# Two pauses in the scatters of rows 16 to 31 of an attention and expert kernel

## The chip, the cores and the metric

The kernel runs on one core of one Trainium2 chip. The metric is the device time of one execution in microseconds (us); where several executions are compared, the median is taken. A core has a matrix engine (PE, with its weight loads shown apart as PEld), three engines for element-wise work (DVE, ACT, POOL), and a queue engine for transfers (SP). ACT and POOL issue transfers too. All transfers run on the same 16 DMA engines of the core.

## The reference

The input holds 4 images of 32 channels, 128 x 128. Each is folded into a matrix of 128 channels by 4096 positions, or 4096 tokens of 128 values as the second layer sees it. Cut to what matters:

```python
# layer 0: attention between channels
q = xs.reshape(B, 128, 4096)
energy = jnp.einsum('bci,bcj->bij', q, q)        # 4096 x 4096 per image
d = jnp.sqrt(jnp.diagonal(energy, axis1=1, axis2=2))
attn = jax.nn.softmax(energy / (d[:, :, None] * d[:, None, :]), axis=-1)
x = gamma * jnp.einsum('bcj,bij->bci', q, attn) + xs
# layer 1: linear attention, then 2 of 8 experts for each token
t = tokens(x)
t = t + linear_attention(layernorm(t), Wk, Wq, Wv)
n = layernorm(t)
top_p, top_i = top_k(softmax(n @ router_w + router_b), 2)
top_p = top_p / sum(top_p)
t = t + sum over the two of  top_p * (n @ expert_w[top_i] + expert_b[top_i])
```

## The kernel before

**Attending.** `attend(b)` walks over the 4096 x 4096 energies of image b in tiles of 128 x 512, row block after row block (0 to 7). One step makes the energies of a tile on PE (`pe`, L556), their exponentials on ACT (`pr`, L559), and two steps later their product with the values (`po`, L440). The energies are symmetric, so only the tiles up to the diagonal are made. The transposed part of a tile goes another way: DVE transposes `pr` in blocks into `F` (L369), SP stores F to DRAM as `blocks` (L483), SP loads it back in another order as `G`, in four quarters (L491), and PE multiplies it (`pg`, L375) while ACT sums its rows (`junk`, L380). The products with G stand LAG = 57 units of the kernel's own clock behind the load. In the last row block of the last image F goes to G directly, in 16 transfers (L476).

**Closing.** When 84% of an image is attended, `layer1(b)` starts as a second stream. Every PACE = 10 units of the clock it makes one step, a "turn" in what follows, while the same image and then the next one are attended. It divides and adds (`close_rows`, L700 to L744), forms the linear attention, and then runs four threads, `attention_rows(u)` for 8 rows of 128 tokens each, started one after another. Threads 1 and 3 end in `sorted_experts(0)` for rows 0 to 15 and `sorted_experts(1)` for rows 16 to 31, for images 0 to 2. Image 3, the last, has no next image to hide behind and multiplies all tokens with all experts instead (`last_parts`).

**Sorting.** `sorted_experts(h)` handles 16 rows with two choices each, 32 pieces. It computes the place of each token in a list ordered by expert, and scatters the 32 pieces to DRAM with indexed transfers from POOL (L995, `xs`), two for every two turns. Each scatter waits for the exponentials of its step. When the thread has issued all, it notes "moved". Then 20 pairs of tiles are loaded by SP (L1019), transposed (L1062) and multiplied by the expert's weights (L1055) on PE, copied by ACT and DVE (L1029, L1038) and stored by SP (`ys`, L1041). At last POOL gathers 32 pieces back (L1120, `yb`), DVE adds them in with their weights (L1089, "combine"), for groups of four rows whose sum starts with a fetch on ACT's queue (`acc`, L1096) and ends with four stores on SP (L1102). Rows 16 to 31 do not start their scatters before rows 0 to 15 have "moved" and do not gather before those have "gathered"; rows 0 to 15 do not gather before rows 16 to 31 have "moved".

**Order.** The orders of PE, DVE, ACT and SP are those in which the program issues its instructions (`manual_schedule`); on POOL the gathers, scatters and small chains are kept in order too (`pinned`). All streams are interleaved by the clock, which counts matmul work, and not by measured time. A pause moves what follows in its thread against all other work, and with it the place in each engine's list. The threads of `stagger` each make a step per turn.

The transfers of SP and ACT draw their completion semaphores from a ring of eight, in the program's order, so a transfer waits until the one eight places ahead of it has landed. The groups of four rows take turns in three `acc` tiles, so a fetch waits for the stores of the group three before. The POOL scatters and gathers have a ring of eight of their own.

Of the kernel before, what the change touches and what calls it, by code (L numbers as in the profile page):

```python
# [22 lines left out]
def kernel(  # L23
# [105 lines left out]
    def wait_for(inst, others, why):  # L129
        for other in others:  # L130
            tc.add_manual_dep(
                inst, other.name, mybir.DependencyInfo(mybir.DependencyClass.Sync, mybir.DependencyReason.DATA),
                reason=why,
            )
# [24 lines left out]
    def pinned(inst):  # L159
        tc.keep_in_program_order(inst)  # L160
        return inst
# [16 lines left out]
    def idle(n):  # L178
        for _ in range(2 * n):
            yield  # L180
# [421 lines left out]
    def layer1(b, st):  # L602
# [276 lines left out]
        def attention_rows(u):  # L879
# [32 lines left out]
            if u % 2:  # L912
                for _ in route(u // 2):
                    yield
                    yield
                yield
                yield
                yield from sorted_experts(u // 2)

        def sorted_experts(h):  # L920
# [66 lines left out]
            def offset(ap):  # L987
                return bass.IndirectOffsetOnAxis(ap=ap, axis=0)
# [4 lines left out]
            for n in range(2 * HR):  # L993
                k, i = r0 + n // 2, n % 2
                inst = nc.gpsimd.indirect_dma_start(xs[h], offset(place[:, i, k : k + 1]), xn[:, k, :], None)  # L995
                if not scatters:
                    pinned(inst)
                else:
                    tc.declare_no_dep(inst.ins, group=f"scatter_{b}_{h}", reason="no two tokens have the same place")
                tc.add_to_no_dep_group(f"scatter_{b}_{h}", inst.ins)  # L1000
                wait_for(inst.ins, xs_made[h] + xs_read[h], "what is replaced was made and read before")
                wait_for(inst.ins, exps, "not more of these at a time than steps have")
                scatters.append(inst.ins)
                if n % 2:
                    yield
                    yield
            turns[h].append("moved")
            xs_made[h][:], xs_read[h][:] = scatters, []
            yield from idle(3)
# [402 lines left out]
```

## Time and profile before

| what | value |
|---|---|
| five runs | 1725.01, 1728.0, 1727.58, 1729.35, 1726.7 us, median 1727.58 |
| the profiled execution | 1721.76 us, span 1720.0 us, granted clock 0.99 |
| busy, share of the span | PE 96%, DVE 54%, ACT 54%, POOL 30% |
| scatters L995 | 192, 968 ns each on POOL |
| gathers L1120 | 192, 962 ns each on POOL |
| transfers | 355.25 MB, 207 GB/s over the span |

A busy time is how long an engine's instructions ran. A row of 40 digits cuts the span into 40 equal parts, each with its busy share in tenths. A wait is named by the engine and line that waited and by what it waited for. "SPq" and "ACTq" are the queues from which SP and ACT issue transfers. Issuing and moving are two things: the time shown beside an issue is that of the engine's queue. Times such as 708.64 us count from the start of the span. In image 0 the scatters of rows 16 to 31 lie at 552 to 604 us, the gathers of rows 0 to 15 at 655 to 707 us and those of rows 16 to 31 from 709 us on; images 1 and 2 repeat this some 412 and 820 to 825 us later.

### The profile page before, as it was taken

Reading aid. Unit: us, or ns where it says so; the run is one execution under the profiler, and the core shown is the slowest. Engines: PE = TensorE matmul, PEld = TensorE weight load, DVE = VectorE, ACT = ScalarE, POOL = GpSimd, SP = SyncE. Lnnn points to the kernel's source line nnn. Section 1 sums busy time; section 2 is a strip of 40 time slices with the busy share of each in tenths; the row PEclk is TensorE's granted clock in tenths of the full one; section 3 lists DMA queues with packets and bytes.
Section 4 is the critical chain, followed back from the end, with each engine's and each line's share of the span. In section 5 each row is a group of like instructions: output and inputs, shape, how many; then the busy total and the mean of one; then the engine's idle time right before and its main releaser. Section 6 shows DMA issues by size and latency. Waiting matters only on the chain. (4 is left out here: it accounts for less than half of the span.)

```text
span 1720.0 us, 21208 instructions
## 1 busy us (share of the span) xinstructions
PE 1656.7 (96%) x5458; PEld 877.8 (51%) x5458; DVE 934.4 (54%) x2443; ACT 925.8 (54%) x2893; POOL 510.4 (30%) x553
## 2 busy tenths in 40 slices
PE   8999999999999999999999999999999999999897
PEld 4444444455654455445554455544555445544643
DVE  4433334467585235577478334557748633455686
ACT  3545445466565455446565545545657545544476
POOL 1000000011026505540015631653102661354156
PEclk9999999999999999999999999999999999999999
DMA  4675777866569899995569879998557979996001
GB/s 134 197 208 171 205 221 236 260 207 184 176 194 269 248 257 263 260 259 164 160 195 243 266 221 258 282 254 232 173 157 193 277 237 259 268 262 161 1 10 41
DMA packets 240681, 355.25 MB, mean 207 GB/s; under 512 B 27312, under 2 KB 155312, under 8 KB 226480
## 3 DMA queue, kind: packets, MB, share of 16 engines
q1 hardware_dynamic: 220048, 314.91, 64.2%
q0 software_dynamic: 12288, 25.19, 5.0%
q10 hardware_dynamic: 8224, 13.77, 2.7%
q8 instruction: 46, 0.75, 0.2%
q14 instruction: 75, 0.61, 0.1%
HBM read 183.64 MB, written 173.15 MB: 207 GB/s over the span
## 5 line engine op out<-in xcount | busy, mean ns | idle before, releaser
L559 ACT ACTIVATE pr<-pe 128x512 f32<-128x512 f32 (+1 forms) x576 | 322.4, 560 | 566.8 <-PE pe L556 433.8
L440 PE MATMUL po<-pr,qT 128*128 128x512 f32 (+3 forms) x1152 | 554.3, 563 | 3.9 <-ACT o L445 3.4
L556 PE MATMUL pe<-qn,qn 128*128 128x512 f32 x896 | 461.9, 597 | 4.2 <-ACT pr L559 3.9
L375 PE MATMUL pg<-G,qT 128*128 128x512 f32 x880 | 452.3, 596 | 9.4 <-DMA G<-blocks 9.4
L369 DVE STREAM_TRANSPOSE F<-pr 128x512 f32<-128x512 f32 x440 | 306.0, 702 | 154.6 <-ACT pr L559 130.8
L440 PEld LDWEIGHTS po<-pr,qT 128*128 128x128 f32 x1152 | 216.7, 192 | 251.2 <-issue 225.2
L380 ACT ACTIVATE junk<-G 128x512 bf16<-128x512 f32 x440 | 272.9, 620 | 2.9 <-DMA G<-blocks 2.6
L375 PEld LDWEIGHTS pg<-G,qT 128*128 128x128 f32 x880 | 167.7, 192 | 208.8 <-issue 192.5
L1120 POOL DMA_INDIRECT yb<-ys,place x192 | 184.8, 962 | 261.4 <-DMA ys<-result 97.2
L995 POOL DMA_INDIRECT xs<-xn,place x192 | 185.8, 968 | 133.0 <-ACT pr L559 55.7
L556 PEld LDWEIGHTS pe<-qn,qn 128*128 128x128 f32 x896 | 154.6, 191 | 116.1 <-issue 102.9
L385 DVE TENSOR_TENSOR o<-o,pg 128x512 f32<-128x512 f32 x110 | 75.4, 685 | 208.8 <-PE pg L375 162.7
L164 POOL TENSOR_TENSOR rn<-ss,neg_half 128x8 f32<-128x8 f32 (+1 forms) x17 | 26.9, 1585 | 333.4 <-DVE ss L325 333.3
L559 ACT ACTIVATION_READ_ACCUMULATOR pr<-pe 128x1 f32 x576 | 112.1, 195 | 0.0
L1029 ACT ACTIVATE xn<-pys 128x256 f32<-128x256 f32 (+1 forms) x120 | 45.0, 378 | 111.9 <-PE pys L1062 63.5
L1055 PEld LDWEIGHTS pys<-ew_sb,xn 128*128 128x128 f32 x468 | 68.9, 193 | 54.8 <-issue 39.6
L164 POOL TENSOR_TENSOR rsf<-dm_f,neg_half 128x8 f32<-128x8 f32 (+1 forms) x15 | 26.2, 1747 | 235.2 <-DVE sv_f L636 235.2
L556 PE MATMUL pe<-qn 128*128 128x512 f32 (+3 forms) x256 | 90.9, 438 | 0.7 <-ACT qn L344 0.7
L164 POOL TENSOR_TENSOR rsa<-dm_a,neg_half 128x8 f32<-128x8 f32 x16 | 26.4, 1649 | 218.0 <-DVE sv_a L636 217.7
L380 ACT ACTIVATION_READ_ACCUMULATOR junk<-G 128x1 f32 x440 | 84.3, 192 | 0.0
L1055 PE MATMUL pys<-ew_sb,xn 128*128 x468 | 71.9, 277 | 10.0 <-ACT xn L1029 9.6
L1038 DVE COPY result<-pys 128x256 f32<-128x256 f32 (+1 forms) x60 | 24.6, 410 | 97.3 <-ACT xn L1029 41.8
(212 smaller groups left out, 1606.9 us busy)
## 6 DMA issues: line engine op xcount, KB each, us to landing
blocks<-F SPq DMA_DIRECT2D x108, 1024.0 KB
G<-blocks SPq DMA_DIRECT2D x432, 256.0 KB
xn<-xs SPq DMA_DIRECT2D x114, 128.0 KB
below<-F SPq DMA_DIRECT2D x31, 384.0 KB
G<-below SPq DMA_DIRECT2D x124, 96.0 KB
out_dram<-acc SPq DMA_DIRECT2D x128, 64.0 KB
xx<-in_x_dram SPq DMA_DIRECT2D x62, 128.0 KB
ys<-xn SPq DMA_DIRECT2D x60, 128.0 KB
```

The source lines that it names most:

```text
L164: pinned(nc.gpsimd.tensor_tensor(dst, src, neg_half.to_broadcast(list(src.shape)), ALU.pow))
L369: f()
L375: nc.tensor.matmul(pg.rearrange("p (a f) -> p a f", a=4), st["qT"][i][:, ib, :], G[:, :, ib], start=(ib == 0), stop=(ib == NJ - 1),)
L380: nc.scalar.activation(junk, G[:, :, ib], AF.Copy, accum_out=st["sums"][:, NJ * i + ib, jc : jc + 1])
L385: nc.vector.tensor_tensor(o, o, pg.rearrange("p (a j c) -> p a j c", a=4, c=S), ALU.add)
L440: nc.tensor.matmul(row["po"][:, lo:hi], qT[blk // NJ][:, blk % NJ, :], w, start=start, stop=(row["left"] == 0))
L556: nc.tensor.matmul(pe[:, c0:], qn[jc][:, ts(j, P)], qn[i][:, c0:], start=True, stop=True)
L559: nc.scalar.activation(pr[:, c0:], pe[:, c0:], AF.Exp, accum_out=sums[:, t, i : i + 1]).ins
L995: inst = nc.gpsimd.indirect_dma_start(xs[h], offset(place[:, i, k : k + 1]), xn[:, k, :], None)
L1029: nc.scalar.activation(bufs[4 + g % 2][:, :n], p[:, : n * P].rearrange("p (j t) -> p j t", t=P), AF.Copy)
L1055: nc.tensor.matmul(p[:, 2 * P + j * D : 2 * P + j * D + D], bufs[4 + g % 2][:, j, :], weights[:, bass.ds(begins[2 * (g % 2) + j], D)], sta ...
L1120: inst = nc.gpsimd.indirect_dma_start(yb[k // 4][:, i, k % 4, :], None, ys, offset(place[:, i, k : k + 1]))
```

## The change

In `sorted_experts`, after the 8th and the 16th scatter, the thread of rows 16 to 31 (h == 1) lets four turns pass without issuing anything. `idle(n)` yields 2n times. Rows 0 to 15 and the number of instructions are as before.

```diff
@@ -1004,6 +1004,8 @@
                 if n % 2:
                     yield
                     yield
+                if h == 1 and n in (7, 15):
+                    yield from idle(2)
             turns[h].append("moved")
             xs_made[h][:], xs_read[h][:] = scatters, []
             yield from idle(3)
```

## The prediction

> **What bounds the kernel now.** I read the page first, then the waits of PE, then windows around the scatters and the gathers, then the order of the DMA issues in the two places where PE waits for a transfer.
>
> ```profile
> PE 1656.7 (96%) x5458; PEld 877.8 (51%) x5458; DVE 934.4 (54%) x2443; ACT 925.8 (54%) x2893; POOL 510.4 (30%) x553
> PE   8999999999999999999999999999999999999897
> DMA  4675777866569899995569879998557979996001
> ```
>
> The page: PE works 96% of the span, so a change that adds no work can only win what is left between its matmuls. The DMA row has its long stretches of 9 where an image closes while the next one is attended.
>
> ```profile
> PE pys L1055 <- ACT xn L1029: 9.6, 3, 3.4
> PE pg L375 <- DMA G<-blocks: 9.4, 5, 2.9
> PE ptq L313 <- DMA xx<-in_x_dram: 9.1, 3, 5.7
> PE pe L556 <- ACT pr L559: 3.9, 5, 1.6
> ```
>
> The waits of PE (total, times, longest). The first line is one hold per image in the products of rows 0 to 15, at 576.7, 992.1 and 1400.6 us, while rows 16 to 31 are scattered. In the second, three of the five are at one place of the image, in the gathers of rows 16 to 31: 2.85 us at 725.8, 1.57 at 1137.9, 2.57 at 1545.4, together 7.0.
>
> ```profile
> 576.00:580.00 4.00, 0.68 (x2) 0.00 (x0) 0.00 (x0) 0.39 (x2) 1.15 (x2) 0.98 0.10 33
> 655.00:708.00 53.00, 52.23 (x192) 29.04 (x191) 30.15 (x70) 27.90 (x86) 30.74 (x31) 1.00 0.93 261
> 708.00:764.00 56.00, 50.03 (x122) 22.60 (x121) 37.49 (x90) 24.09 (x74) 33.74 (x35) 0.94 0.93 261
> 764.00:860.00 96.00, 95.17 (x348) 53.96 (x347) 56.50 (x149) 57.52 (x182) 8.06 (x9) 1.00 0.60 172
> ```
>
> Windows (length, then PE, PEld, DVE, ACT, POOL, granted clock, DMA share, GB/s). In the hold everything stands, transfers too. The gathers of rows 16 to 31 lie in the third window, where PE loses 6 us; behind it the transfers have air.
>
> ```profile
> 706.61 1.82 SPq L491 DMA_DIRECT2D G<-blocks  x4
> 708.53 0.38 SPq L483 DMA_DIRECT2D blocks<-F  x1
> 708.64 0.33 ACTq L1096 DMA_DIRECT2D acc<-t  x1
> 709.01 9.44 SPq L1102 DMA_DIRECT2D out_dram<-acc  x4
> 718.62 0.34 SPq L491 DMA_DIRECT2D G<-blocks  x1
> 728.69 1.10 PE L375 MATMUL pg<-G,qT 128*128 128x512 f32 x2 [2.85 <-DMA G<-blocks]
> ```
>
> The timeline says why G was late. SP needs 9.44 us for four stores that take 1.8 elsewhere (729.93): the fourth shares a completion semaphore with the fetch of acc that ACT issued at 708.64 (eight are handed round over all transfers of SP and ACT), and the fetch landed 8.56 us later. The loads of G stand behind it on SP.
>
> **The change.** It adds no instruction; the counts of every engine are the same. It adds eight turns to the thread that sorts rows 16 to 31, for images 0 to 2. In the program's order of before and after, scatters 8 to 15 move by 24 units of the kernel's clock, scatters 16 to 31 and all behind them (loads, products, stores, gathers, fetches, combines, output stores) by 48 to 56: four or five steps of the stream of exps, 12 to 13 us. The sum is made against the profiled execution, 1721.76 us; the median of the five shown is 1727.58, 5.8 higher, and I add the sum to that.
>
> 1. *The pauses themselves.* POOL issues a scatter each 1.27 us there (0.96 busy, 0.30 issue), and PE waits for none. The image's first wait behind them is the load of rows 16 to 31, at 618 us, 14 us after the last scatter. Rows 0 to 15 wait for "moved" of rows 16 to 31 before they gather, but their own products end later (unit 2644 against 2480, after 2528), so that stays covered: 0. Unless the scatters cause the hold (rival B), bounds 0 and -9.6.
> 2. *The store blocked by the fetch.* The fetches of rows 16 to 31 move behind the stores of group 2, so the block at 709 to 718 us goes. What is late next is blocks<-F: issued at 708.53, 1 MB behind the 1 MB of G before it, at 261 GB/s 8.0 us, landed about 716.5 (an estimate), against 718.6 now: 2.1 us of the 2.85. Image 1: its fourth store left at 1127.5 and G at 1130.5, so it already waits for the blocks: 0. Image 2: blocks at 1527.6, landed about 1535.6 against 1539.0: all 2.57. Together -4.7; bounds -7.0 and 0. The next blocks are hidden: the fetch that now stands at 720 us shares its semaphore with the last quarter of xx, which leaves at 729.4 instead of 726.0 behind a queue that is still full, and PE needs it at 734.3 (0; at most +3 in images 0 and 1 each).
> 3. *The fetch before blocks of the last row.* In before, the fourth fetch of rows 0 to 15 (697.98, landed 4.1 us later) blocked a store at 702.7, issued after blocks<-F of the last row (700.10). With the loads and stores moved among them, the transfer eight places behind that fetch is now those blocks themselves: they leave at 702.1 instead of 700.1, in images 1 and 2 at 1113.2 instead of 1111.1 and 1521.0 instead of 1518.3. Their G is used 7.0 to 8.0 us after its last quarter is issued (708.0 to 715.3 in image 0), and where PE waited, landing took 7.1 to 7.6, so slack is 0 to 1. SP was held until 702.1 anyway, and G then waits for either; I take a third of the delay, 0.7 per image, +2.0. Bounds 0, and +17 with every such fetch as slow as the slowest of this half (7.3 us, at 683.6).
> 4. *Loads of rows 16 to 31* behind the first two fetches: the 7th and the 11th now leave 4 to 7 us late. They have a lead of 13 us to their transposes, at least 6 stays, and loads of before with leads of 4.4 and 5.0 made PE wait for nothing: 0, at most +1 per image.
> 5. *POOL and DVE.* The small chains on POOL (1.6 us each) stand behind fewer gathers, 16 for 24 and 22 for 30. Pairs of combines (0.35 us each) move among the same work, at the two places where PE waits for DVE (754.6 and 1166.6 us) with the same one pair ahead: 0, bounds -0.7 and +0.7 per image.
> 6. *The tail.* Image 2's gathers end 12 us closer to the last attended row. Gained: the last fetch held ACT's queue at 1572.2 us behind a store and cost PE 1.56 us; an earlier fetch stands there now. Lost: DVE has no free stretch from 1594 to 1606 us, where PE waits 2.10 us for rdx, and one pair now lies ahead of it (+0.7), another in the chain to the next rsa (+0.6). Sum -0.3, bounds -1.6 and +5, if the last fetch holds ACT again.
>
> Sum: -4.7 + 2.0 - 0.3 = -3.0, so 1724.6.
>
> [...]
>
> **Rivals.**
> A, slower: step 3 decides. For it: the fetch would run with five more pairs of loads and stores than before, as the one that took 7.3 us did. Against: the three of before took 4.1, 3.7 and 3.9. It decides from a landing above about 5 us, where the delay outgrows the slack; at 7.3 us the blocks leave 5.2, 5.7 and 6.1 us late, 17.0 together, 14.0 less 1 us of slack each, and with steps 2 and 6 +9.0: 1736.6.
> B, faster: the scatters cause the hold of 9.6 us. For it: POOL issues without a pause up to it, and the profile names no cause but "remote". Against: it comes behind scatter 18, 20 and 18 of the 32 but at the same step of the attended stream in all three images, and PE's program is unchanged there. -3.0 - 9.6: 1715.0.
> C, nothing: fetches land early enough to block nobody (then step 3 is 0), and what step 2 frees is taken up by blocks that land later (then step 2 is 0). For it: image 1, where the block was not the last wait. Against: the 9.44 us above. -0.3 alone: 1727.3.
> [...]
>
> **How the numbers follow.** 0.2% is 3.5 us, about what a measurement of this kernel can tell from no change. Forecast 0.42, with its own range from 1718.5 (step 2 at -7.0, step 3 at 0, step 5 at -0.6 each) to 1729 (step 2 at 0): 0.20 of it is faster by over 3.5 us, 0.21 within, 0.01 slower. A 0.30, slower. B 0.12, faster. C 0.16: 0.12 within, and 0.04 slower, with the +5 of step 6. Together faster 0.32, same 0.33, slower 0.35. As cases of both signs hold most of this, the forecast leads only as the largest of four. The range reaches from near B (1716.5) to near A (1736.5).
>
> **What would show it.** Right: the stretch at 709 us has four output stores in about 2 us and the wait of pg near 726 us is under 1 us in images 0 and 2 (step 2); blocks<-F of the last row leaves behind the fetch at 698 us, and pg does not wait at 715 us (step 3); no pys waits for DMA (step 4); the pe wait at 1572 us is gone and the one for rdx is near 2.8 us (step 6). Wrong: a pg wait at 715 us of several us is A; no L1055 hold, or one at another place, is B.

## The result

The changed kernel is a little faster: 1718.73 us median against 1725.92, ratio 0.9962 with a 95% interval of 0.9952 to 0.9972. That is 6.6 us by the ratio, where -3.0 us was forecast (1724.6). The forecast was added to the median of five executions, 1727.58; against the 1725.92 of the 62 in the pair it would be 1722.9. The measured time lies in the range, at the edge of the forecast's own (1718.5 to 1729), and the sign is right. The gain, though, comes from the cause that the prediction gave 12 in 100, rival B, as the experiments show.

The two profiles alone would not tell the sign. The profiled execution of the changed kernel took 1724.78 us, 6 above its median; that of the kernel before took 1721.76, 4 below its median. So the lines below are read for where PE waits, and not for their sum.

The page of the changed kernel, busy time and share of the span:

```profile
PE 1655.0 (96%) x5458; PEld 876.9 (51%) x5458; DVE 934.4 (54%) x2443; ACT 925.4 (54%) x2893; POOL 510.8 (30%) x553
```

The waits of PE in the changed kernel (total, times, longest; its lines behind L1006 are two higher than before):

```profile
PE ptq L313 <- DMA xx<-in_x_dram: 10.2, 3, 5.8
PE pe L556 <- ACT pr L559: 5.5, 5, 2.8
PE pg L375 <- DMA G<-blocks: 5.0, 3, 2.7
...
PE ptq L313 <- issue: 4.1, 1, 4.1
...
PE pgram L676 <- issue: 3.3, 1, 3.3
PE pys L1064 <- DMA xn<-xs: 3.2, 2, 1.9
...
PE pbd L722 <- DVE rdx L700: 2.8, 1, 2.8
...
PE pys L1057 <- ACT xn L1031: 0.8, 2, 0.4
```

The hold of the expert products is gone, 9.6 us down to 0.8. The wait for G has fallen from 9.4 to 5.0. The wait for xx in image 1 (the ptq line with "issue") has grown from 2.1 to 4.1 us. New are one of 3.3 at pgram, 3.2 for the loads of rows 16 to 31, 0.7 more at rdx, and one of 2.8 at pe (770.6 us).

The timeline of the changed kernel at the place where the store was blocked, queues of SP and ACT:

```profile
704.80 1.89 SPq L491 DMA_DIRECT2D G<-blocks  x4
...
707.21 0.47 SPq L483 DMA_DIRECT2D blocks<-F  x1
...
708.23 3.98 SPq L1104 DMA_DIRECT2D out_dram<-acc  x4
712.74 0.89 SPq L1043 DMA_DIRECT2D ys<-result  x2
715.47 1.74 SPq L491 DMA_DIRECT2D G<-blocks  x4
718.68 0.33 ACTq L1098 DMA_DIRECT2D acc<-t  x1
```

The four stores take 3.98 us instead of 9.44, G leaves at 715.47 instead of 718.62, and no wait of pg stands near 726 us any more. A little later, SP and PE in the same kernel:

```profile
718.19 9.74 SPq L279 DMA_DIRECT2D xx<-in_x_dram  x3
728.03 1.91 SPq L1104 DMA_DIRECT2D out_dram<-acc  x4
730.59 0.72 PE L313 MATMUL ptq<-ident,xx 128*128 128x128 f32 x4 [2.57 <-DMA xx<-in_x_dram]
```

The fetch that ACT issued at 718.68 landed 8.00 us later and now holds a load of xx instead of a store. Where the old wait was for G, the new one is for xx.

### The profile page after: what moved, and what is told of

The parts are those of the page before. It is cut to its first block, busy times and chain, and to the rows that moved or that the text cites. A ratio compares the mean times of both kernels' runs of the same rounds, so it can differ in the third digit from the quotient of the medians.

```text
span 1723.0 us, 21189 instructions
## 1 busy us (share of the span) xinstructions
PE 1655.0 (96%) x5458; PEld 876.9 (51%) x5458; DVE 934.4 (54%) x2443; ACT 925.4 (54%) x2893; POOL 510.8 (30%) x553
## 5 line engine op out<-in xcount | busy, mean ns | idle before, releaser
L1031 ACT ACTIVATE xn<-pys 128x256 f32<-128x256 f32 x120 | 45.2, 376 | 112.7 <-PE pys L1064 74.1
L1040 DVE COPY xn<-pys 128x256 f32<-128x256 f32 x60 | 25.4, 423 | 89.2 <-ACT xn L1031 67.6
```

The costliest lines, as they stand in the source:

```text
L1040: nc.vector.tensor_copy(result[:, :n], p[:, 2 * P : 2 * P + n * D].rearrange("p (j c) -> p j c", c=D))
```

## The experiments

Two theories were put to the chip. Theory 1, order: the gain comes from what stands behind the scatters, moved by 12 to 13 us. Theory 2, hold: it comes from the scatters themselves, since an unbroken row of them brings the L1055 hold.

**Only the shift.** The scatters as before, and the eight turns waited behind the last of them.

```diff
-            yield from idle(3)
+            yield from idle(7 if h == 1 else 3)
```

> No pause between the scatters; instead the thread of rows 16 to 31 waits eight turns longer after its last scatter (idle(7) for idle(3)), so everything behind the scatters stands in the same places of all lists as in the changed kernel, and the scatters as in the kernel before. Theory 1, order (the gain comes from what stands behind the scatters, moved by 12 to 13 us): as the changed kernel, 0.9962, holds of L1055 as it pleases. Theory 2, hold (the gain comes from the spread scatters, which take away the hold of PE at L1055, 9.6 us and a lower clock behind each): the holds are back, 9 to 14 us worse than the changed kernel, so 1.001 to 1.004 of the kernel before.

**Only the spread.** Six turns of pause among the scatters, and the six behind them left out, so that what follows stays where it was.

```diff
+                if h == 1 and n in (7, 15):
+                    yield from idle(2 if n == 7 else 1)
...
-            yield from idle(3)
+            yield from idle(0 if h == 1 else 3)
```

> The scatters paused by four turns behind the eighth and two behind the sixteenth, and the six turns after the last scatter left out, so loads, products, gathers, fetches and stores stand where they stood before. Theory 1, order: 1.000 of the kernel before, the pg wait near 726, 1138 and 1545 us as before. Theory 2, hold: no L1055 hold, 9 to 14 us faster, 0.992 to 0.995.

**One pause each.**

```diff
-                if h == 1 and n in (7, 15):
+                if h == 1 and n == 7:      # in the other kernel: n == 15
```

> Only the pause behind the eighth scatter. All behind it moves by about half of the changed kernel's. Theory 2, hold: the hold comes at scatter 18 to 20; with four turns of pause ahead of it there are five scatters less by then, and the hold is gone or moved: 0.993 to 0.998. Theory 1, order: half the shift puts the fetches at other places of the ring of eight, so anything from 0.997 to 1.003, with the L1055 hold still there.

> Only the pause behind the sixteenth scatter, that is two scatters before the hold of the kernel before. Theory 2, hold: no scatters in the four turns in which the hold came, so it is gone: 0.993 to 0.998. Theory 1, order: as the run with the first pause only, since everything behind the scatters moves by the same, 0.997 to 1.003, with the L1055 hold still there.

Measured together on one chip, the kernel before at 1709.13 us: the shift 1.0035 (1.0021 to 1.0049), the spread 1.0001 (0.9988 to 1.0014), the first pause alone 1.0033 (1.0020 to 1.0046), the second alone 1.0047 (1.0034 to 1.0060). Both theories missed. Nothing gained, and theory 1 was off by the sign. But the kernel before ran 17 us faster here than in the pair on record, and the shift, whose scatters are those of the kernel before, showed no L1055 hold. So the hold was not there to be removed.

The semaphore events of the trace show what differs. In the profile of the kernel before, PE's completions come 19 times in a bunch, two to five within 0.2 us, though their matmuls had ended one after another; in that of the changed kernel 16 times. Each comes among POOL's indexed transfers or at most 2.3 us after one, never in the long stretches without any. Records are missing there too: 1372 completions for 1588 matmuls that give one. In these four profiles there is no bunch at all, and at most one record is missing. Unbroken rows are longer here, 19 scatters and up to 26 gathers, and no product waits for ACT behind them. So a long row alone does not bring the hold.

The two kernels with one pause show another cost. The tail of the run with the second pause alone, SP, ACT and PE:

```profile
1565.86 5.97 SPq L1104 DMA_DIRECT2D out_dram<-acc  x12
1569.39 0.37 ACTq L1098 DMA_DIRECT2D acc<-t  x1
1569.81 0.60 ACT L559 ACTIVATE pr<-pe 128x512 f32<-128x512 f32 x1 [10.32 <-DMA out_dram<-acc]
...
1571.54 1.86 PE L676 MATMUL pgram<-xn 128*128 128x128 f32 x7 [6.52 <-ACT xn L644]
```

Image 2's last fetch waits in ACT's queue for stores that SP issues only behind its transfers of G, ACT stands still for 10.32 us, and PE loses 6.52. With the first pause alone it is 11.05 and 7.25.

**All four again, on another chip.** The changed kernel, the kernel before, the shift and the spread, unchanged, measured together.

> The changed kernel as it is. In the four runs so far no profile shows the bursts in which PE's completions come late and together, and with them no L1055 hold; in the blind pair both kernels show them at several places. Theory 2, hold: where the kernel before shows the L1055 hold, the changed kernel is 0.994 to 0.998 of it; where it does not, the changed kernel wins nothing, 1.001 to 1.005, as the run that only shifts. Theory 1, order: 0.996 in either case.

> The kernel before, for its profile beside the others of this call. Theory 2: L1055 waits of about 3 us at the 18th to 20th scatter of rows 16 to 31 if the times are near 1726 us, and none if they are near 1709. Theory 1 says nothing about it. Time 1.000.

> The run that only shifts, again, beside the changed kernel. Theory 2: behind the changed kernel by 9 to 14 us if the kernel before shows the L1055 hold here, equal to it within 3 us if not. Theory 1: equal to it within 3 us.

> The run that only spreads the scatters, again. Theory 2: 0.992 to 0.995 if the kernel before shows the L1055 hold here, 1.000 if not, as measured before. Theory 1: 1.000.

Here the kernel before took 1728.18 us, and its profile has waits at the products again, 7.0 us in five, the longest 4.1. Against it: the changed kernel 0.9944 (0.9920 to 0.9967), the shift 1.0050 (1.0024 to 1.0076), the spread 0.9906 (0.9878 to 0.9934). The kernel before again was 1.0000 (0.9981 to 1.0018). Theory 2 holds in its direction: the shift loses 0.5%, the spread wins 0.94%, and the changed kernel, which does both, wins 0.56%. The shift is far from the changed kernel, 18 us by the medians (1737.86 and 1719.81), though all that stands behind the scatters has the same places in both. Both effects are larger than theory 2 had them (9 to 14 us, and 0.992 to 0.995 for the spread).

The waits of PE at the expert products, first the run with only the shift, then that with only the spread:

```profile
PE pys L1055 <- ACT xn L1029: 12.2, 5, 3.8
```

```profile
PE pys L1057 <- ACT xn L1031: 0.6, 1, 0.6
```

One hold from near, timeline of the run with only the shift:

```profile
576.97 0.61 PE L1055 MATMUL pys<-ew_sb,xn 128*128 x4
...
579.30 0.96 POOL L995 DMA_INDIRECT xs<-xn,place  x1 [0.30 <-issue]
580.21 0.61 PE L1055 MATMUL pys<-ew_sb,xn 128*128 x4
580.57 0.96 POOL L995 DMA_INDIRECT xs<-xn,place  x1 [0.30 <-issue]
581.84 0.96 POOL L995 DMA_INDIRECT xs<-xn,place  x1 [0.30 <-issue]
582.38 1.02 PE L375 MATMUL pg<-G,qT 128*128 128x512 f32 x2
583.10 0.96 POOL L995 DMA_INDIRECT xs<-xn,place  x1 [0.30 <-issue]
586.10 0.38 ACT L1029 ACTIVATE xn<-pys 128x256 f32<-128x256 f32 x1 [6.11 <-remote]
586.54 1.22 PE L1055 MATMUL pys<-ew_sb,xn 128*128 x4 [3.14 <-ACT xn L1029]
587.23 0.96 POOL L995 DMA_INDIRECT xs<-xn,place  x1 [3.17 <-ACT pr L559]
```

POOL issues ten transfers without a break, the last at 583.10. PE's products of 580.2 us are done, but the copies on ACT that need them start at 586.10; PE waits for ACT, and POOL for the exponentials of ACT. The row of scatters ends at 584.06, and the completions come at 586.08, 2.0 us later. At the holds of all the profiles with bunches this delay is 1.8 to 2.5 us, behind rows of 10 to 14. Not every such row costs PE time: in the kernel before, rows of 11 and 10 scatters just ahead of the first hold end in bunches too (547.2 and 561.6 us), and PE does not wait there. The same place in the run with only the spread:

```profile
575.80 0.96 POOL L995 DMA_INDIRECT xs<-xn,place  x1 [0.30 <-issue]
575.95 0.38 ACT L1031 ACTIVATE xn<-pys 128x256 f32<-128x256 f32 x1 [1.08 <-issue]
577.78 0.96 POOL L995 DMA_INDIRECT xs<-xn,place  x1 [1.02 <-issue]
578.33 0.61 PE L1057 MATMUL pys<-ew_sb,xn 128*128 x4
579.04 0.96 POOL L995 DMA_INDIRECT xs<-xn,place  x1 [0.30 <-issue]
580.94 0.38 ACT L1031 ACTIVATE xn<-pys 128x256 f32<-128x256 f32 x1 [2.83 <-PE pe L556]
581.38 0.71 PE L1057 MATMUL pys<-ew_sb,xn 128*128 x4
```

POOL stops in the pause, the completions come, and PE goes on without a wait. The hold cost more than its 3.14 us of idle time. Two windows of the run with only the shift, then of that with only the spread (length, PE, PEld, DVE, ACT, POOL, granted clock, which is the share of its full speed that PE was given, DMA share, GB/s):

```profile
583.00:587.00 4.00, 0.86 (x3) 0.47 (x3) 0.48 (x2) 0.90 (x4) 0.96 (x1) 0.89 0.88 207
587.00:590.00 3.00, 3.00 (x10) 2.18 (x10) 1.69 (x7) 1.87 (x7) 1.92 (x2) 0.58 0.88 307
```

```profile
583.00:587.00 4.00, 4.00 (x17) 2.41 (x16) 1.12 (x5) 2.11 (x9) 0.96 (x1) 1.00 1.11 346
587.00:590.00 3.00, 3.00 (x14) 1.88 (x13) 0.78 (x2) 1.60 (x5) 1.95 (x3) 1.00 0.86 271
```

Behind the hold the granted clock is 0.58 for 3 us, and the same 3 us hold 10 matmuls instead of 14. The clock's records show half speed behind each of the three long L1055 holds of that run, from 586.1, 995.7 and 1412.2 us on, for 3.41, 6.83 and 3.41 us. The idle gaps are 3.14, 3.81 and 3.70 us, 10.65 together; with half of 13.65 lost, 6.8, the three holds cost some 17.5 us, an estimate. The changed kernel, whose order behind the scatters is the same, is 18 us faster by the medians. The length of the gap alone does not decide: in the first profile of the kernel before, one of 2.96 us (992.1) is followed by such a stretch, of 3.41 us, and one of 3.25 us (1400.6) is not. Within each of the two profiles of the pair all the stretches begin whole multiples of 3.413 us apart (in the kernel before the next three 44, 52 and 122 of them after the first, which begins at 579.8 us); whether it matters how a gap lies on this grid was not tested.

Over the whole profiles of these four, the waits of PE (idle gaps over 0.15 us) and the time lost at half clock: kernel before 64.5 and 15.5 us, changed 53.0 and 20.3, shift 64.5 and 23.9, spread 52.0 and 9.8, with spans of 1731.8, 1721.9, 1736.5 and 1712.4. Less these two, the four spans lie within 1648.1 to 1651.9 us. From the shift to the changed kernel the waits at the products fall from 12.2 to 1.5 us, nearly all of the difference in waits. From the kernel before to the spread they fall by 6.4, half of it; the other half is scattered over many lines, and that execution of the kernel before was 5 us above its median.

**The place of the pause, and where the shift's cost lies.** The same six turns behind the 24th scatter, where the hold has already come:

```diff
-                if h == 1 and n in (7, 15):
-                    yield from idle(2 if n == 7 else 1)
+                if h == 1 and n == 23:
+                    yield from idle(3)
```

> The same six turns as in the run that only spreads the scatters, taken in one pause behind the 24th scatter, and the turns after the last scatter left out as there; all that stands behind the scatters is where it was before. In the kernel before, the L1055 hold comes when POOL has issued 10 to 14 indexed transfers without a break, at scatter 18 to 20, ahead of this pause. Theory 2, hold by unbroken scatters: the hold stays, so 1.000 where the spread run had 0.9906, with L1055 waits of 3 to 4 us in two or three images. If only the mean rate of the scatters counted, or the turns left out at the end, it would be 0.990 to 0.995 as the spread run. On a chip without the bursts of late completions: 1.000 by every theory.

The shift, but not for image 2:

```diff
-            yield from idle(7 if h == 1 else 3)
+            yield from idle(7 if h == 1 and b < 2 else 3)
```

> The run that only shifts, but not for image 2, whose gathers reach into the last row of the last image. Shifting all three cost 1.0035 and 1.0050. If the tail carries that cost (last fetch in ACT's queue, combines ahead of rdx), this is 0.999 to 1.001; if each image carries its third (xx waits near 730 and 1138 us, transposes L1062 that wait for loads), it is 1.0023 to 1.0033.

These two ran on a chip without bunches (before 1711.37 us): the late pause 0.9992 (0.9979 to 1.0005), so its question stayed open; the shift without image 2 1.0006 (0.9994 to 1.0018), no loss that can be told from none. Shifting all three had cost 1.0035 on another chip without bunches. By these two ratios most of the shift's cost hangs on image 2, whose last fetch and combines run into the last rows. Which waits carry it stays open: the profile of the shift on a chip without bunches has only 0.65 us more at rdx, in an execution 4.6 us below its median.

**The place once more, and even pauses.** The late pause again, and three pauses of two turns instead of four and two:

```diff
-                if h == 1 and n == 23:
-                    yield from idle(3)
+                if h == 1 and n in (7, 15, 23):
+                    yield from idle(1)
```

> The one pause behind the 24th scatter again, since the chip of the last call showed no bursts in either profile. Where the kernel before runs near 1726 us (bursts): theory 2 has 0.998 to 1.002 with the L1055 waits still there, the mean rate alone 0.990 to 0.995. Near 1709 us: 1.000, and the question stays open.

> The same six turns in three pauses of two, behind the 8th, 16th and 24th scatter, and the turns after the last left out. Where the kernel before shows bursts: no unbroken run of rows 16 to 31 is longer than 8 to 10 and the L1055 hold is gone, 0.989 to 0.995; with pauses too short to empty POOL's list the hold stays, 0.997 to 1.001. On a chip without bursts 1.000.

On a chip with bunches (before 1728.13 us) the late pause is 1.0002 (0.9980 to 1.0023), the even pauses 0.9930 (0.9908 to 0.9952). The waits at the products, late pause first:

```profile
PE pys L1057 <- ACT xn L1031: 8.9, 5, 3.8
```

```profile
PE pys L1057 <- ACT xn L1031: 2.7, 3, 1.0
```

So it is the place that counts. Six turns behind the hold win nothing, and the mean rate of the scatters, equal in both, is not the cause. Two turns at each of three places are enough for most of the gain, but the hold is not quite gone: rows of 10 scatters remain in this run, and PE loses 1.0 us behind two of them (582.7 and 991.0 us).

The version with only the spread is the best of the four on the chip with bunches, 0.9906 where the changed kernel is 0.9944, and costs nothing that can be told on a chip without, 1.0001. Whether the changed kernel gains on such a chip was not run; its two halves were, 1.0035 and 1.0001, and speak against it.

## Why the prediction was right or wrong

**Step 1, the pauses themselves.** Taken at 0, with -9.6 as the far bound; the far bound it was. The argument against rival B was that the hold comes at the same step of the attended stream in all three images while the number of scatters differs, 18, 20 and 18. As far as the runs show, what counts is the unbroken row ahead of the products and not the number: the rows before those holds were 12, 10 and 12 transfers long. And 9.6 was too small a price: two of the three holds were followed by 3.41 us at half clock each (from 579.8 and 996.3 us), which was in no term.

**Step 2, the blocked store.** Right in the mechanism and the time: the block went, G left 3.1 us earlier, and the wait near 726 us with it, also in images 1 and 2. Wrong in what it called hidden. The last quarter of xx waited for the fetch and left at 727.62, 1.8 us sooner than forecast; but PE was there at 728.02 and not at 734.3, since the hold and the wait for G ahead of it were gone, 3.4 and 2.9 us. It lost 2.57 us in image 0, and in image 1 4.05 instead of 2.08; both lie within the bound of +3. A wait for G of 1.25 us (738.6) is new too. Of the 7.0 us of old waits, 7.0 less 2.57, 1.97 and 1.25 leaves 1.2, and not 4.7; the half clock behind waits (3.41 us from 730.0 us on in the kernel before) is not in this sum, and the granted clock differs from one execution to the next (0.985 to 0.995 in the 20 of the kernel before beside the even pauses).

**Step 3, the fetch before the last row's blocks.** Forecast +2.0, measured 0: the blocks took the place behind the fetch, but the fetch landed after 3.94, 4.00 and 3.73 us, in image 0 at 697.5, the blocks left at 698.05, and PE had no wait at 715 us. Rival A did not come.

**Step 4, the loads of rows 16 to 31.** Taken at 0, with +1 per image as the bound; PE waited 1.93 us in image 1 and 1.31 us in image 2, both above the bound. The leads of the 7th and the 11th load fell to 7.5 to 9.6 us, as forecast (at least 6), and PE waited for neither. It waited for the 12th in image 1 and the 15th in image 2, which had leads of 8.2 us. The step looked at two loads out of twenty. Why these two landed so late stays open, as the 16th and 17th had leads of 4.3 to 4.9 us and PE did not wait.

**Step 5.** The waits at the two places are 1.57 instead of 2.55 and 3.09 instead of 3.07; right within its bounds except for the first, which is 0.3 us better than its bound.

**Step 6, the tail.** The wait for rdx grew from 2.10 to 2.75 as forecast (+0.7). The hold of ACT did not go away but moved: the last fetch stood for 4.4 us at 1579.5, instead of 5.6 at 1572.2, and PE lost 3.35 us at pgram where it had lost 1.56. So in this profile the tail costs 2.4 us, and -0.3 should have been above zero; the repeat of the changed kernel lost 0.4 at pgram. The bound of +5 held it, and the run that leaves image 2 out of the shift, with no loss to be told from none, points to the tail too.

Together: the sum of -3.0 has the sign of the measured -6.6 only by two errors that partly cancel, and that is luck. The order behind the scatters, held for a gain, costs 0.35 to 0.5%; the spread of the scatters, held for nothing, wins 0.94% on a chip with bunches. Fetches that block nobody, the first half of rival C, are not what the profiles show: the 24 fetches land after 2.6 to 9.4 us in the kernel before and after 2.3 to 8.9 us in the changed one, where the xx load behind the fetch of 718.68 us could not leave before 727.62.

## What to carry to other kernels

A wait whose releaser is called "remote", while the engine that should release it has long issued its work, deserves an experiment before it is priced at nothing: here the completions were late, 2.0 us behind the row of scatters in the run with only the shift, and not the work. Try to keep indexed transfers on POOL in short rows, with gaps ahead of the places where PE, ACT and POOL wait for each other, and put the gaps so that what stands behind does not move: here, with bunches, the waits at the products were 7.0 us in the kernel before, 0.6 with pauses behind the 8th and the 16th scatter and 8.9 with one behind the 24th. When a change moves a transfer in a ring of semaphores, look up which transfer now stands a round behind it, eight places in this kernel, and when the engine that needs that one will be there in the changed kernel: here PE came to xx at 728.02 and not at 734.3 us, since two waits ahead of it were gone.

## What was not expected

PE's completions came late and in bunches while POOL issued indexed transfers without a break, and in the two profiles of the pair up to 2.3 us after it stopped. This was so on some chips: eight profiles showed 16 to 25 bunches each, with the kernel before at 1726 to 1728 us; six profiles of two other chips showed none, with it at 1709 to 1711 us. Each of the four chips of the experiments was used once, so the chip and the time of the run are not told apart. The changed kernel still has bunches: one of four at 772.86 us, behind ten gathers, ends its new wait of 2.8 us at pe. That POOL's transfers are what holds up PE's completions is argued from their places in time; how, and why only on some chips, stays open, as no run here looks inside. That a pause ahead of the products matters was shown; that the holds at the products lie behind rows of ten transfers or more was only seen in these rows, and need not be a threshold.
